# A fused attention and FFN layer on one core: first x piece in token halves, a shorter run of zero products, a full-tile count, and the float16 products first behind the last value products

## The chip, the cores and the metric

The kernel runs on one core of one Trainium2 chip. The metric is device time in microseconds (us) of that core, the median of several runs. TensorE (PE in the profile) does matrix products and loads its weights separately (PEld); VectorE is DVE, ScalarE is ACT, GpSimd is POOL, and SyncE (SP) issues most of the DMA transfers. A "q" behind an engine's name (SPq, ACTq) is its instruction queue, where transfers are issued.

## The reference

The input x has 4 x 2048 tokens of 256 features. One layer is computed, in float32:

```
Q = x @ W_q.T ; K = x @ W_k.T ; V = x @ W_v.T
S = (Q K^T within chunks of 32 tokens) * mask     # mask[i,j] = decay^(i-j) for i >= j, else 0
O = S V                                           # also within the chunk
attn = (sigmoid(x @ W_g.T) * O) @ W_o.T + x
x = layernorm(x + attn)
h = silu(x @ w_gate.T) * (x @ w_up.T)             # 768 hidden features, integer weights / 127
x = layernorm(x + h @ w_down.T)
```

The decay is the sigmoid of one number. The three FFN weights come as 32-bit integers between -127 and 127.

## The kernel before, in words

The 8192 tokens are worked in 16 blocks of 512 (`TB`). Within a block, features lie on the 128 partitions in two halves (`KD` = 2), and tokens run along the free dimension, or the other way round where the product needs it. The kernel is written out in program order: `in_turn` pins an instruction to its place on its engine, so the order of TensorE's products is what the Python code says.

Precision is kept by splitting. A float32 operand is written as a high part in `fp32r` (one pass on TensorE) and a low part. In attention, blocks 1 to 15 use three products of `fp32r` parts (`three`: parts hi, lo and gap). In the FFN, each product is a pair: high parts in `fp32r`, low parts in float16 (`kind` 0 and 1 in `ffn_up`; the trace names them `fg_hi`, `fg_lo` and so on). Block 0's attention is done with plain float32 products, each of which the trace shows as two matmul instructions.

**The start.** Loads are issued from two queues: SP loads the transposed x of block 0 (`xT`, two pieces of 256 KB, one per feature half), then `wq`, then the x of block 1, `wo`, the untransposed x and the integer weights; ACT loads `wg` in two pieces, `wv`, `decay` and `wk`. TensorE first runs products of zeros, whose widths stand in `WARM`, into a scratch bank `pi` (line 193). Then come the gate products of block 0 (`attn_gate`, `pg`, line 576), half of the value products (`pv`, line 618), the product of W_q and W_k (`make_m`, `pm`, line 216), the other half of `pv`, and `py` (line 597).

**The count.** Some integer weights could be too wide for the split. `wide_counter` compares the maxima of the nine weight pieces with 128 and sums the nine columns of 0 or 1 with one TensorE product `pw` (line 311) against a column of ones. It sits on TensorE between the transposes `pt` of block 0 (line 809) and the gap products `p_o` of block 1 (line 512). If the count is over zero, a slow path at the end runs.

**The loop.** For block b the loop does the FFN up-products of block b in six chunks of 128 hidden features (`hc` 0 to 5; `ffn_up`, line 879), and between them the attention of block b + 2 and b + 3: the scores `ps` (line 652), the values `po` (`attn_values`, line 688, products on a quarter of the array), the gate and value products; then the down-product `fdn` (line 734). In `ffn_up` the variable `kinds` sets which parts come first:

```
kinds = (1, 0) if hc % 2 or low_first else (0, 1)
```

so even chunks take high before low, odd chunks low before high, and two neighbouring chunks meet in the same type. For the blocks with `more` (b up to 12) chunk 4, which follows `attn_values`, is called with `low_first=True`. Block 13 is the last pass of the loop (`not more`): there the value products of block 15 stand between chunk 1 and chunk 2, and chunk 2 takes its high parts first. After the loop come blocks 14 and 15 and a hand-written tail of normalizing and storing.

Of the kernel before, what the change touches and what calls it, by code (L numbers as in the profile page):

```python
# [47 lines left out]
F32 = mybir.dt.float32  # L48
# [4 lines left out]
ALU = mybir.AluOpType  # L53

P = 128
# [3 lines left out]
TB = 512  # L59
NG = TB // P  # L60
HB = TB // 2
# [8 lines left out]
SHIFT = 2.0**12  # L70
TOP = 1.0 - 0.5 / SHIFT
WHOLE = 1.0 + 1.0 / SHIFT
WARM = 512, 256, 128


@with_exitstack
def kernel(
# [15 lines left out]
    nc = tc.nc  # L93
    NT, D = x.shape
    H = ffn_gT.shape[1]
    KD = D // P
# [4 lines left out]
    const = ctx.enter_context(tc.tile_pool(name="const", bufs=1))  # L101
# [12 lines left out]
    def in_turn(ins):  # L114
        tc.keep_in_program_order(ins)

    def bank(name):
        return psum.tile([P, TB], F32, tag="ps", name=name)


    def span(b, start):
        return slice(b * TB, (b + 1) * TB) if start is None else bass.ds(start, TB)

    def queue(start):

        return nc.sync if start is None else nc.gpsimd

    def load_xT(b, start=None, pieces=1):
        xt = xin.tile([P, KD, TB], F32, tag="xT", name=f"xT_{b}")
        src = xT[:, span(b, start)].rearrange("(k p) t -> p k t", p=P)  # L130
        n = KD // pieces
        for k in range(0, KD, n):
            queue(start).dma_start(xt[:, k : k + n, :], src[:, k : k + n, :])
        return xt

    def load_xn(b, start=None):
# [5 lines left out]
    def load_w(eng, w, name, pieces=1):  # L142
        k, n = w.shape[0] // P, w.shape[1]
        t = const.tile([P, k, n], w.dtype, tag=name, name=name)
        per = k // pieces
        for i in range(0, k, per):
            eng.dma_start(
                t[:, i : i + per, :], w.rearrange("(k p) n -> p k n", p=P)[:, i : i + per, :]
            )
        return t  # L150
# [2 lines left out]
    decay = const.tile([P, 1], F32, tag="decay", name="decay")  # L153
    xTs, xns = {}, {}
    wg = load_w(nc.scalar, w_gT, "wg", pieces=KD)
    xTs[0] = load_xT(0, pieces=KD)
    wv = load_w(nc.scalar, w_vT, "wv")
    nc.scalar.dma_start(decay, log_decay[0:1, 0:1].to_broadcast([P, 1]))
    wq = load_w(nc.sync, w_q, "wq")
# [31 lines left out]
    pi = bank("pi")  # L191
    for n in WARM:
        nc.tensor.matmul(
            pi[:, :n],
            lhsT=nc.const_aps.tensor(0.0, [P, P]),
            rhs=nc.const_aps.tensor(0.0, [P, n]),
            start=True,
            stop=True,
# [6 lines left out]
    half = const.tile([P, NG], F32, tag="half", name="half")  # L205
# [82 lines left out]
    top = const.tile([P, n_pieces], F32, tag="top", name="top")  # L288
# [13 lines left out]
    def wide_counter():  # L302

        wide = const.tile([P, top.shape[1]], F32, tag="wide", name="wide")
        in_turn(nc.vector.tensor_scalar(wide, top, EXACT, None, ALU.is_gt))
        ones = const.tile([P, 1], F32, tag="ones", name="ones")
        nc.vector.memset(ones, 1.0)

        def count_wide():
            pw = bank("pw")[:1, : top.shape[1]]  # L310
            in_turn(nc.tensor.matmul(pw, lhsT=ones, rhs=wide, start=True, stop=True))
            count = const.tile([1, 1], F32, tag="count", name="count")
            in_turn(nc.vector.tensor_reduce(count, pw, mybir.AxisListType.X, ALU.add))
            return count

        return count_wide
# [7 lines left out]
    def in_steady_turn(ins):  # L324
        if steady:
            tc.keep_in_program_order(ins)
# [233 lines left out]
    def split_v(b, x_parts):  # L560
        v = work.tile([P, NG, D], F32, tag="v", name=f"v_{b}")
        per = TB // D

        def finish(i, pb):
            in_turn(nc.scalar.copy(flat(v, slice(i * per, (i + 1) * per)), pb))

        return v, three(f"v_{b}", token_major(w_parts["wv"], x_parts), finish)

    def attn_gate(b):
        xt = xTs[b]  # L570
        sg = work.tile([P, KD, TB], F32, tag="sg", name=f"sg_{b}")
        banks = [bank(f"pg_{b}_{dc}") for dc in range(KD)]

        for ec in range(KD):
            for dc, pg in enumerate(banks):
                product = nc.tensor.matmul(  # L576
                    pg,
                    lhsT=given["wg"][:, ec, dc * P : (dc + 1) * P],
                    rhs=xt[:, ec, :],
                    start=(ec == 0),  # L580
                    stop=(ec == KD - 1),
                )
                in_turn(product)
        def gate():
            for dc, pg in enumerate(banks):
                in_turn(nc.scalar.activation(sg[:, dc, :], pg, AF.Tanh, scale=HALF))

        return sg, gate
# [275 lines left out]
    def no_more_splits():  # L864
        while late_splits:
            late_splits.pop(0)()

    def ffn_up(b, hT, uT, chunks, cols=slice(0, TB), held=False, low_first=False):

        n = cols.stop - cols.start  # L870
        for hc in chunks:
            pg = bank(f"fg_{b}_{hc}_{cols.start}")[:, :n]
            pu = bank(f"fu_{b}_{hc}_{cols.start}")[:, :n]

            kinds = (1, 0) if hc % 2 or low_first else (0, 1)
            for kind in kinds:
                for pb, w in ((pg, fg), (pu, fu)):
                    for dc in range(KD):
                        product = nc.tensor.matmul(  # L879
                            pb,  # L880
                            lhsT=w[kind][:, dc, hc * P : (hc + 1) * P],
                            rhs=hT[kind][:, dc, cols],
                            start=(kind == kinds[0] and dc == 0),
                            stop=(kind == kinds[1] and dc == KD - 1),
                        )
                        in_turn(product)
            s = work.tile([P, n], F32, tag="s", name=f"s_{b}_{hc}")
            in_turn(nc.scalar.activation(s, pg, AF.Silu, scale=SCALE / H_UP))  # L888
            no_more_splits()
            if len(uT[0]) == hc:  # L890
                for kind, dtype, tiles in zip(("hi", "lo"), (F32R, F16), uT):
                    tiles.append(
                        acts.tile([P, TB], dtype, tag=f"u_{kind}", name=f"u_{kind}_{b}_{hc}")
                    )

            def multiply(hc=hc, pu=pu, s=s):
                u = work.tile([P, n], F32, tag="u", bufs=3, name=f"u_{b}_{hc}")
                in_steady_turn(
                    nc.vector.scalar_tensor_tensor(u, pu, U_UP / H_UP, s, ALU.mult, ALU.mult)  # L899
                )  # L900
                hi, lo = uT[0][hc][:, cols], uT[1][hc][:, cols]

                def split():
                    in_steady_turn(nc.scalar.copy(hi, u))  # L904
                    in_steady_turn(nc.gpsimd.tensor_tensor(lo, u, hi.bitcast(F32), ALU.subtract))  # L905

                if lagging:
                    late_splits.append(split)
                else:
                    split()  # L910

            if held:
                return multiply
            multiply()
# [159 lines left out]
    count = count_wide()  # L1074
# [5 lines left out]
    def up_now(b, hT, uT, hc):  # L1080
        ffn_up(b, hT, uT, range(hc, hc + 1))
# [19 lines left out]
    for b in range(NB - 2):  # L1101
        n = b + 2
        m = b + 3
        more = m < NB
# [3 lines left out]
        hT = hTs.pop(b)  # L1108
        uT = ([], []) if b else uT_0
# [6 lines left out]
        multiply = ffn_up(b, hT, uT, range(1, 2), held=True)  # L1116
# [11 lines left out]
            multiply()  # L1128
        if not more:
            goT = attn_values(n, sT, v, sg)  # L1130
        multiply = ffn_up(b, hT, uT, range(2, 3), held=True)
        if b > 1:
            normalize(r_before, *scales_out, range(NG // 2))
        multiply()
# [4 lines left out]
            moving = move_h(b + 1, hs[b + 1])  # L1139
        if not more:  # L1140
            go_parts, go_gaps = token_parts(goT, f"go_{n}")
        multiply = ffn_up(b, hT, uT, range(3, 4), held=True)
        if b > 1:
            normalize(r_before, *scales_out, range(NG // 2, NG))
        multiply()
# [2 lines left out]
        if more:  # L1148
            sT_next = attn_scores(m, yT)
            goT = attn_values(n, sT, v, sg)  # L1150
            multiply = ffn_up(b, hT, uT, range(4, 5), held=True, low_first=True)
            go_parts, go_gaps = token_parts(goT, f"go_{n}")
            if b == 0:
                cast_fd(1, range(1))
            multiply()
            go_gaps()
            v_next, v_rest = split_v(m, x_parts)
            sg_next, g_rest = split_gate(m, x_parts)
            v_rest()
            if b == 0:  # L1160
                cast_fd(1, range(1, 2))
            up_with_cast(b, hT, uT, 5, 1, range(2, 3))
        else:
            up_now(b, hT, uT, 4)
            go_gaps()
        r_before = r_out
        if more:
# [26 lines left out]
        else:  # L1194
            multiply = ffn_up(b, hT, uT, range(5, KH), held=True)
# [19 lines left out]
    per = NG // 2  # L1215
    cols = [slice(i * per * P, (i + 1) * per * P) for i in range(2)]
    uT_last = [], []
    uT = [], []
# [19 lines left out]
    for i in range(2):  # L1238
        groups = range(i * per, (i + 1) * per)
        multiply = ffn_up(last - 1, hTs[last - 1], uT, range(3 + i, 4 + i), held=True)  # L1240
# [263 lines left out]
    with tc.If(wide_any > 0, preferred_fallthrough_block=False):  # L1504
# [10 lines left out]
        for w in (ffn_gT, ffn_uT, ffn_dT):  # L1515
            weights.append([])
            for src in int_pieces(w):
                t = room.pop(0).rearrange("p (k n) -> p k n", n=D)
# [52 lines left out]
```

## Time and profile before

| what | value |
|---|---|
| median of 3 runs | 489.17 us (489.13 to 489.43) |
| the profiled execution's own time | 489.44 us |
| its span, first to last instruction | 487.8 us |
| mean granted TensorE clock over the span | 0.999 |
| TensorE busy | 481.4 us, 99% of the span |
| ACT, DVE, POOL busy | 374.5, 338.7, 281.2 us |
| TensorE busy after 482.40 us | 0.13 us |

The profile is one execution. A row of the timeline gives a start, a duration, the engine, the line, the operation, output and inputs, and a count where equal neighbours were merged. Matmuls overlap one another: a row's duration includes the time that a result takes to come out, so the pace of the engine is read from the distance between starts, not from the durations. The waits list who waited for whom, with total, number of times and longest, in us.

### The profile page before, as it was taken

The numbers are of one execution on the slowest core, as the hardware profiler recorded it, in microseconds if no ns is written. First come the engines' busy times: TensorE is split into PE (matmuls) and PEld (weight loads), VectorE is DVE, ScalarE is ACT, GpSimd is POOL, SyncE is SP. The second block draws the span as 40 slices with busy tenths as digits, with TensorE's granted clock in tenths as the row PEclk, the third lists the DMA queues.
The fourth block names the chain that finished last, engine by engine and source line by source line (L and its number), as shares of the span: only waits on it lengthen the run. The fifth ranks groups of instructions, "written<-read, shape, count | busy, mean of one in ns | idle before, by whom it ended". The sixth has DMA issues, their size and how long they took to land.

```text
span 487.8 us, 12289 instructions
## 1 busy us (share of the span) xinstructions
PE 481.4 (99%) x4760; PEld 382.3 (78%) x4760; DVE 338.7 (69%) x795; ACT 374.5 (77%) x699; POOL 281.2 (58%) x285
## 2 busy tenths in 40 slices
PE   9999999999999999999999999999999999999995
PEld 5787787887868878687887868878687887868674
DVE  4687958687575876757677575875757677567656
ACT  4878687687877878688687877878688787786845
POOL 3835755555735565464555735566465555657764
PEclk9999999999999999999999999999999999999999
DMA  8820411211403123131411403123132211103102
GB/s 258 253 92 7 131 45 51 80 46 42 133 22 110 44 59 118 31 101 54 118 47 39 134 25 110 45 80 94 27 105 54 79 44 38 53 20 112 35 14 83
DMA packets 43323, 36.99 MB, mean 76 GB/s; under 512 B 4864, under 2 KB 39168, under 8 KB 43264
## 3 DMA queue, kind: packets, MB, share of 16 engines
q1 hardware_dynamic: 42144, 35.28, 24.4%
q10 hardware_dynamic: 1120, 0.92, 0.6%
q8 instruction: 38, 0.62, 0.5%
q14 instruction: 21, 0.17, 0.1%
HBM read 20.45 MB, written 8.39 MB: 59 GB/s over the span
## 4 chain that ended last, share of the span: by engine, by line
PE 98%; DMA 1%; DVE 0%; ACT 0%; issue 0%
PE fg L879 18%; PE fu L879 18%; PE fdn L734 14%; PE p_v L512 9%; PE p_o L512 9%; PE p_y L490 9%; PE p_g L490 9%; PE po L688 4%; PE ps L652 2%; PE fdn L953 2%; PE fdn L1313 1%; PE pg L576 1%; DMA wg<-in_w_gT_dram 1%; PE pa L767 1%; PE pv L618 1%; PE py L597 1%
## 5 line engine op out<-in xcount | busy, mean ns | idle before, releaser
L905 POOL TENSOR_TENSOR u_lo<-u,u_hi 128x512 f16<-128x512 f32 (+1 forms) x98 | 129.4, 1325 | 96.5 <-ACT u_hi L904 95.4
L899 DVE SCALAR_TENSOR_TENSOR u<-fu,s 128x512 f32<-128x512 f32 (+1 forms) x98 | 66.1, 675 | 84.7 <-ACT s L888 82.5
L888 ACT ACTIVATE s<-fg 128x512 f32<-128x512 f32 (+1 forms) x98 | 57.4, 585 | 48.1 <-PE fg L879 48.1
L904 ACT CAST u_hi<-u 128x512 fp32r<-128x512 f32 (+1 forms) x98 | 59.4, 606 | 32.8 <-DVE u L899 32.8
L879 PE MATMUL fg<-hT_hi,fg_hi 128*128 128x512 f32 (+1 forms) x196 | 72.4, 451 | 0.0
L879 PE MATMUL fu<-hT_hi,fu_hi 128*128 128x512 f32 (+1 forms) x196 | 60.5, 390 | 0.0
L879 PE MATMUL fg<-hT_lo,fg_lo 128*128 128x512 f16 (+1 forms) x196 | 58.2, 379 | 0.0
L879 PE MATMUL fu<-hT_lo,fu_lo 128*128 128x512 f16 (+1 forms) x196 | 57.5, 375 | 0.0
L471 POOL TENSOR_TENSOR go_lo<-goT,go_hi 128x512 fp32r<-128x512 f32 x30 | 44.6, 1506 | 18.2 <-ACT go_hi L470 18.2
L477 DVE SCALAR_TENSOR_TENSOR go_gap<-go_hi,goT 128x512 fp32r<-128x512 f32 x30 | 48.2, 1645 | 0.8 <-ACT go_hi L470 0.7
L471 POOL TENSOR_TENSOR x_lo<-xT,x_hi 128x512 fp32r<-128x512 f32 x30 | 37.8, 1283 | 14.6 <-ACT x_hi L470 14.6
L734 PE MATMUL fdn<-fd_hi,u_hi 128*128 128x256 f32 x312 | 44.6, 285 | 0.0
L879 PEld LDWEIGHTS fg<-hT_hi,fg_hi 128*128 128x128 f32 x196 | 35.7, 190 | 10.3
L879 PEld LDWEIGHTS fu<-hT_hi,fu_hi 128*128 128x128 f32 x196 | 36.6, 188 | 8.4
L788 DVE TENSOR_TENSOR h<-p_o,x 128x512 f32<-128x512 f32 x30 | 19.3, 685 | 32.8 <-PE p_o L512 28.9
L734 PEld LDWEIGHTS fdn<-fd_hi,u_hi 128*128 128x128 f32 x312 | 38.9, 188 | 0.3
L734 PE MATMUL fdn<-fd_lo,u_lo 128*128 128x256 f16 x312 | 38.6, 274 | 0.0
L856 POOL TENSOR_TENSOR hT_lo<-hT,hT_hi 128x512 f16<-128x512 f32 x28 | 35.4, 1284 | 4.3 <-ACT hT_hi L855 4.3
L879 PEld LDWEIGHTS <-fu_lo 128*128 128x128 f16 x196 | 19.2, 98 | 22.2
L734 PEld LDWEIGHTS <-u_lo 128*128 128x128 f16 x312 | 28.4, 98 | 3.9
L424 ACT ACTIVATE h<-h,shift_h,scale_h 128x256 f32<-128x256 f32 x52 | 27.0, 589 | 2.2 <-DVE shift_h L387 0.8
L879 PEld LDWEIGHTS <-fg_lo 128*128 128x128 f16 x196 | 13.1, 98 | 19.2 <-issue 12.8
(175 smaller groups left out, 1042.7 us busy)
## 6 DMA issues: line engine op xcount, KB each, us to landing
x<-in_x_dram SPq DMA_DIRECT2D x16, 512.0 KB, 3.9
xT<-in_xT_dram SPq DMA_DIRECT2D x15, 512.0 KB, 4.7
hT<-sq SPq DMA_DIRECT2D x224, 32.0 KB, 1.9
out_dram<-r SPq DMA_DIRECT2D x13, 512.0 KB, 3.3
out_dram<-r SPq DMA_DIRECT2D x7, 128.0 KB, 1.7
fg_int<-in_ffn_gT_dram SPq DMA_DIRECT2D x3, 256.0 KB, 7.9
fu_int<-in_ffn_uT_dram SPq DMA_DIRECT2D x3, 256.0 KB, 7.1
fd_int<-in_ffn_dT_dram SPq DMA_DIRECT2D x3, 256.0 KB, 5.9
```

The source lines that it names most:

```text
L424: nc.scalar.activation(r[:, g, :], r[:, g, :], AF.Identity, bias=shift[:, g : g + 1], scale=scale[:, g : g + 1],)
L471: in_turn(nc.gpsimd.tensor_tensor(lo[:, k, :], t[:, k, :], whole, ALU.subtract))
L477: nc.vector.scalar_tensor_tensor(gap[:, k, :], whole, -WHOLE, t[:, k, :], ALU.mult, ALU.add)
L490: nc.tensor.matmul(pb, lhsT=a[kind][:, k, i * P : (i + 1) * P], rhs=b[kind][:, k, :], start=kind + k == 0, stop=True, skip_group_check=True,)
L512: nc.tensor.matmul(pb[:, j * D : (j + 1) * D], lhsT=b[kind][:, k, g * P : (g + 1) * P], rhs=a[kind][:, k, :], start=kind + k + j == 0, sto ...
L734: product = nc.tensor.matmul(pb[:, j * D : (j + 1) * D], lhsT=part[:, g * P : (g + 1) * P], rhs=w, start=(i == 0), stop=(i == len(terms) - 1),
L856: nc.gpsimd.tensor_tensor(in_order[1], whole, in_order[0].bitcast(F32), ALU.subtract)
L879: product = nc.tensor.matmul(pb, lhsT=w[kind][:, dc, hc * P : (hc + 1) * P], rhs=hT[kind][:, dc, cols], start=(kind == kinds[0] and dc == ...
L888: in_turn(nc.scalar.activation(s, pg, AF.Silu, scale=SCALE / H_UP))
L899: nc.vector.scalar_tensor_tensor(u, pu, U_UP / H_UP, s, ALU.mult, ALU.mult)
L904: in_steady_turn(nc.scalar.copy(hi, u))
L905: in_steady_turn(nc.gpsimd.tensor_tensor(lo, u, hi.bitcast(F32), ALU.subtract))
```

## The change

- `WARM` goes from three zero products (512, 256 and 128 columns) to two (512 and 128).
- The first piece of block 0's `xT` is loaded in two transfers of 256 tokens (128 KB each) instead of one of 512 tokens. The second piece is unchanged.
- The gate products of block 0 that use this piece are done by token halves: four products of 256 columns instead of two of 512. Those of the second piece are unchanged. Only the very first product into a bank starts it; the others add.
- The count's product uses a 128 x 128 tile of the constant 1.0 in place of a 128 x 1 tile `ones` that was filled by a memset; its result then fills 128 partitions, of which the first is read.
- In `ffn_up`, `low_first` now exchanges the order of the parts in even and odd chunks alike, where before it made every chunk low-first. In the last pass of the loop (block 13), chunks 2, 3 and 4 are called with it: low-high, high-low, low-high, instead of high-low, low-high, high-low. For the other blocks nothing changes, since only chunk 4 has the flag there, and it is even.

```diff
-WARM = 512, 256, 128
+WARM = 512, 128
...
-    def load_xT(b, start=None, pieces=1):
+    def load_xT(b, start=None, pieces=1, first_by=1):
         xt = xin.tile([P, KD, TB], F32, tag="xT", name=f"xT_{b}")
         src = xT[:, span(b, start)].rearrange("(k p) t -> p k t", p=P)
         n = KD // pieces
         for k in range(0, KD, n):
-            queue(start).dma_start(xt[:, k : k + n, :], src[:, k : k + n, :])
+            per = TB // (1 if k else first_by)
+            for t in range(0, TB, per):
+                piece = slice(k, k + n), slice(t, t + per)
+                queue(start).dma_start(xt[:, *piece], src[:, *piece])
         return xt
...
-    xTs[0] = load_xT(0, pieces=KD)
+    xTs[0] = load_xT(0, pieces=KD, first_by=2)
...
-        ones = const.tile([P, 1], F32, tag="ones", name="ones")
-        nc.vector.memset(ones, 1.0)
 
         def count_wide():
-            pw = bank("pw")[:1, : top.shape[1]]
+            pw = bank("pw")[:, : top.shape[1]]
+            ones = nc.const_aps.tensor(1.0, [P, P])
             in_turn(nc.tensor.matmul(pw, lhsT=ones, rhs=wide, start=True, stop=True))
             count = const.tile([1, 1], F32, tag="count", name="count")
-            in_turn(nc.vector.tensor_reduce(count, pw, mybir.AxisListType.X, ALU.add))
+            in_turn(nc.vector.tensor_reduce(count, pw[:1, :], mybir.AxisListType.X, ALU.add))
             return count
...
-        for ec in range(KD):
+        halves = [slice(0, HB), slice(HB, TB)]
+        for ec, tokens in [(0, half) for half in halves] + [
+            (ec, slice(0, TB)) for ec in range(1, KD)
+        ]:
             for dc, pg in enumerate(banks):
                 product = nc.tensor.matmul(
-                    pg,
+                    pg[:, tokens],
                     lhsT=given["wg"][:, ec, dc * P : (dc + 1) * P],
-                    rhs=xt[:, ec, :],
-                    start=(ec == 0),
-                    stop=(ec == KD - 1),
+                    rhs=xt[:, ec, tokens],
+                    start=ec + tokens.start == 0,
+                    stop=True,
+                    skip_group_check=True,
                 )
...
-            kinds = (1, 0) if hc % 2 or low_first else (0, 1)
+            kinds = (1, 0) if hc % 2 != low_first else (0, 1)
...
-        multiply = ffn_up(b, hT, uT, range(2, 3), held=True)
+        multiply = ffn_up(b, hT, uT, range(2, 3), held=True, low_first=not more)
...
-        multiply = ffn_up(b, hT, uT, range(3, 4), held=True)
+        multiply = ffn_up(b, hT, uT, range(3, 4), held=True, low_first=not more)
...
         else:
-            up_now(b, hT, uT, 4)
+            ffn_up(b, hT, uT, range(4, 5), low_first=True)
             go_gaps()
```

## The prediction, as it was put on record

> **What bounds the kernel now.** I read the page first, its busy times and its chain.
>
> ```profile
> span 487.8 us, 12289 instructions
> PE 481.4 (99%) x4760; PEld 382.3 (78%) x4760; DVE 338.7 (69%) x795; ACT 374.5 (77%) x699; POOL 281.2 (58%) x285
> ...
> PE 98%; DMA 1%; DVE 0%; ACT 0%; issue 0%
> ```
>
> TensorE is the bound, nearly without a gap: 481.4 of 487.8 us. The last products start at 482.14, and 5.3 us of normalizing and storing follow that no edit touches. So a gain on TensorE passes to the end, and what other engines or queues gain does not count. What can be won lies at the start and in the distances between products. The chain of waits in the first 20 us shows the start:
>
> ```profile
> 0.97 3.46 DMA wg<-in_w_gT_dram
> 4.43 0.04 issue
> 4.47 4.06 PE pg L576 x8
> 8.53 1.73 PE pv L618 x8
> ```
>
> The first real product waits for a transfer, by name the first piece of wg, until 4.43. Before that TensorE multiplies zeros; narrow windows of the timeline show these and the clock:
>
> ```profile
> 1.00 3.32 PE L193 MATMUL pi<-const-float32-0.0 128*128 128x512 f32 x6 [1.00 <-PEq L1556]
> 4.63 0.34 PEld L576 LDWEIGHTS pg<-xT,wg 128*128 128x128 f32 x1
> 5.36 0.19 PEld L576 LDWEIGHTS pg<-xT,wg 128*128 128x128 f32 x1 [0.39 <-issue]
> ```
>
> The same weight load takes 0.34 us at 4.63 and 0.19 at 5.36: until a moment between, TensorE runs at half speed. The PEclk row reads full from the first slice, but the trace's own clock record begins at 5.22 us; its second and last entry is half clock for 3.41 us from 486.5. From 5.22 to 486.5 are 141 times 3.41 us. So the clock is decided at steps of 3.41 us, and 5.22 is the first step after a stretch (1.81 to 5.22) in which TensorE was busy for 3.26 of 3.41 us.
>
> For the other edits I read the timeline at their places: the count,
>
> ```profile
> 43.75 1.03 PE L809 MATMUL pt<-ident,h 128*128 128x128 f32 x8
> 44.71 0.20 PE L311 MATMUL pw<-wide,ones 128*1 128x9 f32 x2
> 44.84 0.62 PE L512 MATMUL p_o<-wo_gap,go_gap 128*128 128x256 f32 x3
> ```
>
> and the products behind the values, in block 13 (high parts first) and in block 12 (low parts first):
>
> ```profile
> 432.10 1.16 PE L688 MATMUL po<-sT,v 64*64 64x64 f32 x64
> 433.19 0.73 PE L879 MATMUL fg<-hT_hi,fg_hi 128*128 128x512 f32 x2
> 433.76 0.63 PE L879 MATMUL fu<-hT_hi,fu_hi 128*128 128x512 f32 x2
> ```
> ```profile
> 409.86 1.16 PE L688 MATMUL po<-sT,v 64*64 64x64 f32 x64
> 410.95 0.60 PE L879 MATMUL fg<-hT_lo,fg_lo 128*128 128x512 f16 x2
> 411.39 0.60 PE L879 MATMUL fu<-hT_lo,fu_lo 128*128 128x512 f16 x2
> ```
>
> **The change part by part.**
>
> *Token halves and gate by halves.* Single packets of the trace: one of 2 KB (a row of xT) holds a DMA engine 84 ns, one of 1 KB (a row of wg) 46 ns, and the SP and ACT queues alternate on each of 16 engines. From 3.0 us, when wg's packets have begun to flow, to 3.845, when its last starts, each engine takes 6.5 rounds of 84 + 46 = 130 ns. With xT rows of 1 KB a round is 92 ns: 0.60 instead of 0.845, so wg lands 0.25 us earlier, at 4.18. The first half of xT has half the bytes of what landed at 4.24 and is there before. The first product then starts at about 4.22 instead of 4.47. Ends: no gain, if the early stalls of the queues decide (up to 0.95 us on single packets); 0.57, if the start moves to 3.9. I take 0.25. Until 5.22 TensorE runs at half speed, so 0.25 us of earlier start is worth 0.13 at the end (0 to 0.29). The gate's first piece becomes eight instructions of 256 columns for four of 512. The 256-column pv rows stand 0.216 us apart at full clock, the 512-column pg rows 0.429: 4 x (0.432 - 0.429) = 0.01 us. Their loads of 0.19 (cold 0.34) hide beneath passes of 0.216 (cold 0.43). The second half's bytes stand next in the queue and land by about 4.6, needed at 5.6; the second piece landed at 5.27, needed at 6.2 or later.
>
> *One transfer more.* SP issues one DMA more (0.4 us of SP); xT's second piece and wq go out 0.44 later. Before, eight transfers go out and the ninth waits for the first landing: SP's queue waits show
>
> ```profile
> SPq L133 <- DMA wg<-in_w_gT_dram: 2.1, 1, 2.1
> ```
>
> With one more in front, wk on ACT's queue can become the ninth and wait until 4.2 instead of going out at 2.90. Behind it on ACT stand the table load (3.41 to 4.69), the one-column Sigmoid (4.70) and wg_hi (5.57): they slip by 1.3, 1.3 and about 0.65 us, and POOL's wg_lo with wg_hi. ACT then idles for the decay until 8.19, and POOL until 11.47, so this is hidden. wk lands at 8.9 and is first loaded at 9.88; its packets stand behind wv's and decay's in the same queue, so an issue 1.3 later shifts it by a few tenths at most. Cost 0; without that cover, see rival 3. The x of block 1 goes out when an early transfer lands, at 4.0 to 4.4 instead of 4.44, and its user x_hi (10.77) is safe. The integer weights are each issued behind another landing, by at most about 1 us; fg_int lands near 16.4 and is first read at 21.1. Cost 0.
>
> *Fewer zero products.* The 256-column product took 0.85 us (starts 2.835 and 3.262, the next at 3.689). The zeros end at 3.47 instead of 4.32. As the data come at 4.22 at the earliest value that I take, this itself frees nothing; it only makes a hole from 3.47 to 4.22. Here a rule weighs against the change. The Trainium skill, "TensorE: Matmul & The Clock Gate", section "Part 1: The HAM clock gate", says that the clock stays half until a window of about 3.4 us, free-running, has been one of sustained activity. The row agrees on the length. It doesn't say how much idling a window may hold. In this trace 24% busy (the window ending at 1.81, with work from 1.00) was too little and 96% was enough; after the change it would be 3.26 - 0.75 + the old hole of 0.15 = 2.66 us, 78%. Read strictly, the rule costs one more window at half speed: 3.41 / 2 = 1.71 us. Read by the row alone, with the point anywhere between 24 and 96%, the chance to miss is (96 - 78) / (96 - 24) = 25%, and 35% if the data come no earlier (71%). I take no loss as the likeliest, and the loss as the main rival.
>
> *The count.* From the last transpose (start 44.509) to the second p_o product (45.067) are 0.558 us: the one-column load starts only at 44.710, when the transposes are through, and p_o's load (0.19) starts together with its product instead of ahead. In a full tile the loads can go ahead as between the transposes, 0.108 us apart: two steps for pw, one for p_o, one of 0.117 make 0.44. Gain 0.11. The same page, section "LDWEIGHTS (loading the stationary operand)", speaks against it: a load takes columns / 1.2 ns, so 128 columns for one is 2 x 106 ns more, a loss of 0.2. The rows have 79 and 82 ns for the one-column loads, so they are not nearly free, and the price lies in the order; I take 0.11 gain, ends -0.2 and 0.12. The memset dropped is 0.06 us of DVE beside the zeros: nothing.
>
> *Float16 behind the values.* The two fg products take 433.756 - 433.188 = 0.568 where high parts come first, and 411.392 - 410.950 = 0.442 where low ones do. An undisturbed high pair takes 0.467 (436.90), a low one 0.432: the high weights' load is exposed by 0.10, the low ones' by 0.01. The rest of the order: chunks 2 to 5 took 1.910 + 1.801 + 1.809 + 1.797 = 7.317 us. From like rows the new order is 1.809 (block 12, chunk 4), 1.809, 1.801, and 1.807 for chunk 5, which now begins with a change of type: 7.226. Gain 0.09. In both orders fg is complete two products before the chunk's end, so ACT and DVE get it as before.
>
> *Sum:* 0.13 - 0.01 + 0.11 + 0.09 = 0.32 us. The profiled execution's 489.44 (span 487.8 and 1.6 around it) becomes 489.12; it stood 0.27 above the median, so the median goes from 489.17 to 488.85.
>
> **The rivals.**
>
> 1. *The clock is released a step late (0.35).* The hole before the first product keeps the window below the point that counts; the next step is at 8.63. Loss 1.71, less the 0.32: 490.56 us, slower. It decides as soon as the point lies above about 78%. For it: the hole grows from 0.15 to 0.75 us, and the skill asks for sustained work. Against it: work covers the larger part on both sides. Its own range is 490.2 to 490.9.
> 2. *The data come no earlier (0.08).* If wg is held by stalls and not by alternation, the start stays at 4.47; only count and values gain, 0.2: 488.97.
> 3. *wk too late (0.06).* If the whole 1.28 us of its later issue reached its landing, it would come at 10.2, and pm, needed 0.13 sooner at 9.75, would hold TensorE 0.45 us: 489.3. For over 0.2% it has to be about 1 us later still (0.02).
> 4. *Other order (0.08).* One more transfer and one memset less can re-plan unpinned instructions, mostly on POOL and SP. No wait of TensorE is there to be removed, so a gain of 1 us has no place that I know: 0.06 above that to the fast side, for what I overlooked; 0.02 slow.
>
> That the order change fails to reach its place is excluded by the code: only chunk 4, an even one, has the flag elsewhere.
>
> **How the numbers follow.** The likeliest is all three gains with the clock on time (0.43): 488.85, own range 488.6 to 489.1. A measurement of this kernel can tell about 0.2%, 0.98 us: below 488.19 is faster, above 490.15 slower. Same: 0.43 + 0.08 + 0.04 of rival 3 = 0.55. Slower: 0.35 + 0.02 + 0.02 = 0.39. Faster: 0.06. The range has to hold rival 1, so it runs from 488.4 (start at 3.9 and both small gains full, 488.67, less the 0.3 by which runs differ) to 490.9.
>
> **What would show it.** The first pg row at 4.2 and not 4.47, and loads of 0.19 from 5.2 on: the start is right. Loads of 0.34 until 8.6 and a later start of pv: rival 1. The p_o product 0.33 us behind the last transpose and the next 0.11 on, and a pair of 0.44 behind po in block 13: the two small gains. A wait of pm's load for wk: rival 3. The prediction is wrong if TensorE's work from 60 to 400 us changes its length, or the tail after the last product.

## The result, and the profile after

The changed kernel is slower: 495.31 us (median of 4 runs, 494.86 to 495.42) against 489.15 (4 runs, 488.90 to 489.43), a ratio of 1.0117 with a 95% interval of 1.0104 to 1.0130. The prediction had 488.85 and a range that ended at 490.9.

The page of the changed kernel, the lines that answer to those of before:

```profile
span 493.1 us, 12292 instructions
PE 484.3 (98%) x4762; PEld 385.0 (78%) x4762; DVE 338.5 (69%) x794; ACT 375.5 (76%) x699; POOL 281.6 (57%) x285
...
PE 96%; DMA 2%; DVE 0%; ACT 0%; issue 0%
```

The bound is still TensorE, but two things grew. Its busy time rose by 2.9 us with two products more. And the chain of waits gives 2% to transfers, where it was 1%. So a part of the loss is waiting, and a part is the same work at a slower pace. They lie in different places.

**The start.** The timeline of TensorE (start, duration, engine, line, operation, output and inputs, count; in brackets the idle time just before, and what ended it):

```profile
3.87 2.72 PE L581 MATMUL pg<-xT,wg 128*128 128x256 f32 x8 [0.39 <-DMA wg<-in_w_gT_dram]
7.41 1.95 PE L581 MATMUL pg<-xT,wg 128*128 128x512 f32 x4 [0.82 <-DMA xT<-in_xT_dram]
9.20 1.89 PE L624 MATMUL pv<-wv,xT 128*128 128x256 f32 x8
11.94 1.99 PE L219 MATMUL pm<-wk,wq 128*128 128x256 f32 x8 [0.85 <-DMA wk<-in_w_k_dram]
```

The first gate product starts at 3.87 instead of 4.47, earlier than forecast. But two waits follow that were not there before: 0.82 us for the second piece of xT, and 0.85 for wk. pv starts at 9.20 (before 8.36) and pm at 11.94 (before 10.09), so the 0.6 us won have become a loss of 1.85. The list of transfers in the first 16 us (transfer, queue, count, KB each, median us from issue to landing) says why:

```profile
xT<-in_xT_dram SPq DMA_DIRECT2D x1, 256.0 KB, 5.4
wk<-in_w_k_dram ACTq DMA_DIRECT2D x1, 256.0 KB, 8.1
```

The first of these is xT's second piece. It takes 5.4 us; before, the two pieces took 3.9 in the median. It went out at 1.86 instead of 1.41 and landed at 7.27 instead of 5.27. wk takes 8.1 instead of 6.0: out at 3.84 instead of 2.90, landed at 11.89 instead of 8.91. The chain of waits up to 16 us (start, duration, what), its middle:

```profile
3.84 8.05 DMA wk<-in_w_k_dram
...
11.94 1.99 PE pm L219 x8
```

wk is now the ninth transfer; it goes out when the first piece of wg has landed, and then it decides the start.

**The loop.** The value products `po` come once in a block, so their starts measure a block's length. Two rows of before, then the same two of after:

```profile
116.46 1.16 PE L688 MATMUL po<-sT,v 64*64 64x64 f32 x64
380.52 1.16 PE L688 MATMUL po<-sT,v 64*64 64x64 f32 x64
```
```profile
118.77 1.16 PE L694 MATMUL po<-sT,v 64*64 64x64 f32 x64
384.69 1.16 PE L694 MATMUL po<-sT,v 64*64 64x64 f32 x64
```

They are nine blocks apart: 264.06 / 9 = 29.340 us a block before, 265.92 / 9 = 29.547 after. Each block takes 0.207 us more, though no edit touches a product in it. The groups of the down-product, high and low parts, before and after the change (busy us, mean ns):

```profile
L734 PE MATMUL fdn<-fd_hi,u_hi 128*128 128x256 f32 x312 | 44.6, 285 | 0.0
L734 PE MATMUL fdn<-fd_lo,u_lo 128*128 128x256 f16 x312 | 38.6, 274 | 0.0
```
```profile
L740 PE MATMUL fdn<-fd_hi,u_hi 128*128 128x256 f32 x312 | 45.6, 288 | 0.0
L740 PE MATMUL fdn<-fd_lo,u_lo 128*128 128x256 f16 x312 | 38.6, 273 | 0.0
```

Only the fp32r rows, here the high parts, are longer. By mean distance between starts (57.58 to 410 us of the span), the high down-products stand 126.2 ns apart instead of 123.0, the value and output products of the attention 119.5 instead of 117.8, the 512-column gate products 233 instead of 231. Float16 products keep their 109 and 216 ns.

From the rows of `po` and the last product the sum is: up to the first `po` (25.42 before, 27.41 after) +1.99; from there to 57.58 (59.47) -0.10; from there to 409.86 (414.35) +2.60; from there to the last products, 482.14 (486.99), +0.36. That is +4.85.

**The end.** The last store takes 3.5 us from its issue to the end of the span instead of 3.1, which makes the span's 5.2. The store itself lands as fast as before, but the span now ends 1.38 us behind its landing instead of 0.96. SP's records show why: at the end SP waits on eight DMA semaphores (counters that a transfer raises when it has landed), in a fixed order and 0.06 us apart. The one that comes last belongs to the last of these eight waits before and to the first of them after, so seven more steps follow the landing. All traces below agree: 1.38 or 1.39 us in the eight kernels that issue one more transfer on SP's or ACT's queue (the changed one, 3, 5, 6, 10, 11, 12 and 13), 0.95 or 0.96 in all others. So the added transfer costs 0.42 us there too.

**The two small edits.** The count, and the products behind block 15's values:

```profile
45.74 1.03 PE L815 MATMUL pt<-ident,h 128*128 128x128 f32 x8
...
46.76 1.07 PE L514 MATMUL p_o<-wo_gap,go_gap 128*128 128x256 f32 x7
```
```profile
437.88 0.60 PE L885 MATMUL fg<-hT_lo,fg_lo 128*128 128x512 f16 x2
438.32 0.59 PE L885 MATMUL fu<-hT_lo,fu_lo 128*128 128x512 f16 x2
```

From the transposes to the gap products are 1.02 us instead of 1.09 (to the second gap product the gain is 0.10), and the first pair behind the values takes 0.44 instead of 0.57. Both small gains are in the trace.

### The profile page after: what moved, and what is told of

The parts are those of the page before. It is cut to its first block, busy times and chain, and to the rows that moved or that the text cites. A ratio compares the mean times of both kernels' runs of the same rounds, so it can differ in the third digit from the quotient of the medians.

```text
span 493.1 us, 12292 instructions
## 1 busy us (share of the span) xinstructions
PE 484.3 (98%) x4762; PEld 385.0 (78%) x4762; DVE 338.5 (69%) x794; ACT 375.5 (76%) x699; POOL 281.6 (57%) x285
## 4 chain that ended last, share of the span: by engine, by line
PE 96%; DMA 2%; DVE 0%; ACT 0%; issue 0%
PE fg L885 18%; PE fu L885 17%; PE fdn L740 15%; PE p_v L514 9%; PE p_o L514 9%; PE p_y L492 9%; PE p_g L492 9%; PE po L694 4%; PE ps L658 2%; PE fdn L959 2%; DMA wk<-in_w_k_dram 2%; PE fdn L1319 1%; PE pa L773 1%; PE py L603 1%; DMA wg<-in_w_gT_dram 1%; PE pm L219 0%
## 5 line engine op out<-in xcount | busy, mean ns | idle before, releaser
L740 PE MATMUL fdn<-fd_hi,u_hi 128*128 128x256 f32 x312 | 45.6, 288 | 0.0
L740 PEld LDWEIGHTS fdn<-fd_hi,u_hi 128*128 128x128 f32 x312 | 39.9, 189 | 0.3
L388 POOL TENSOR_SCALAR minus_out<-rstd_out 128x4 f32<-128x4 f32 x12 | 2.7, 223 | 44.8 <-DVE rstd_out L386 44.8
```

The source lines that it names most:

```text
L740: product = nc.tensor.matmul(pb[:, j * D : (j + 1) * D], lhsT=part[:, g * P : (g + 1) * P], rhs=w, start=(i == 0), stop=(i == len(terms) - 1),
```

## The experiments

The change drops one tile of 4 bytes a partition, `ones`. The addresses in the built programs show what this does: constants that are allocated ahead of it stay, and everything allocated behind it (xT, hT, u, the parts of the sums) lies 32 bytes nearer (xT from 73600 to 73568). The theory for the loop is that this shift alone slows the fp32r products. Its rival is that one of the edits does. For the start the theory is the added transfer; the rivals are named with the runs. Each kernel was timed in turn with the kernel before on the same chip. The release of the clock falls at another moment in each run (3.9 to 7.6 us in most of the traces below), and half of it passes into the time: the kernel before took from 488.84 to 490.51 over all its runs. So tenths of a microsecond are read from the traces, and times only decide from about 0.2% on.

**1 and 2. The kernel before, with later tiles 32 and 64 bytes further.** One unused tile, then two, behind `ones`:

```diff
+        pad = const.tile([P, 1], F32, tag="pad", name="pad")
+        nc.vector.memset(pad, 1.0)
```

> The kernel before with one unused 4-byte tile added behind the tile of ones (and its memset), so that every tile allocated after it lies 32 bytes further on; nothing else changes. Theory A (addresses): the fp32r products between block 1 and block 13 lose what they lost in the changed kernel, about 2.7 us (489.2 to 491.9), and the distances of float16 products stay; the start keeps the order of before: first pg product at 4.47, pm at 10.1. Rival B (the drift follows from the shifted start or from another order of the engines, not from addresses): no change, 489.2. Rival C (the late transfers at the start come from misplaced destinations too): also pm later by 1 to 2 us, 493.5 to 494.

> The same with two unused 4-byte tiles, so that later tiles lie 64 bytes further on. Theory A in the form that the place within 64 bytes decides: no change, 489.2 (within 0.3 us). If any shift of the later tiles against the earlier ones costs, as theory A would also allow: again about 491.9. Rival B: 489.2 here and in the run with 32 bytes.

Measured: 490.18 against 489.78, 1.0008 [0.9999, 1.0016], and 491.05, 1.0033 [1.0020, 1.0045]. Blocks took 29.367 and 29.447 us. Unused tiles alone change the pace, but by other amounts than the shift the other way: the 2.7 us that the theory expected from any 32 bytes did not come.

**3. The changed kernel with the addresses of before.** The same unused tile, put where `ones` was.

> The changed kernel with an unused 4-byte tile (and its memset) in the place of the tile of ones, so that all tiles lie where they lay before. Theory A with the queues as the cause at the start: the drift of 2.7 us is gone, the late second piece of xT (wait of about 1 us) and the late wk (about 1 us) stay: 489.15 + 1.95 - 0.2 = about 490.9 to 491.5. Rival C (destinations make the transfers late): start good too, 488.5. Rival B: 495.3 as the changed kernel.

Measured: 492.09 against 489.78, 1.0053 [1.0041, 1.0066]. The loop is back:

```profile
118.83 1.16 PE L696 MATMUL po<-sT,v 64*64 64x64 f32 x64
236.19 1.16 PE L696 MATMUL po<-sT,v 64*64 64x64 f32 x64
```

Four blocks in 117.36 us are 29.34 each (a single later block took 29.44), and the high down-products are back at 285 ns. The start stays as late as in the changed kernel: wk lands at 12.34 and pm starts at 12.38. So loop and start are two causes, and the loop's goes away with the tile put back.

**4. The small edits alone.** The kernel before with the full-tile count, the unused tile, and the new order in block 13; three zero products and whole pieces stay.

```diff
-        ones = const.tile([P, 1], F32, tag="ones", name="ones")
-        nc.vector.memset(ones, 1.0)
+        pad = const.tile([P, 1], F32, tag="pad", name="pad")
+        nc.vector.memset(pad, 1.0)
...
-            kinds = (1, 0) if hc % 2 or low_first else (0, 1)
+            kinds = (1, 0) if hc % 2 != low_first else (0, 1)
```

> The kernel before with only the full-tile count (and an unused tile in place of the ones, so that addresses stay) and the new order of parts in block 13; three zero products, first piece of xT whole, gate whole. As predicted for these two parts: 0.11 + 0.09 = 0.2 us faster, 488.95. If neither is worth anything: 489.15.

Measured: 489.80 against 489.78, 1.0002 [0.9994, 1.0010], too little for the time to tell. The trace has the count 0.08 faster. Block 15's values need a closer reading. The timeline of this kernel, then of the kernel before, up to the low part of the down-product that follows chunk 5:

```profile
434.10 0.60 PE L885 MATMUL fg<-hT_lo,fg_lo 128*128 128x512 f16 x2
...
444.16 1.05 PE L959 MATMUL fdn<-fd_lo,u_lo 128*128 128x256 f16 x8
```
```profile
443.23 1.05 PE L953 MATMUL fdn<-fd_lo,u_lo 128*128 128x256 f16 x8
```

Chunks 2 to 5 take 7.235 us instead of 7.317, the gain that was forecast. But the 24 fp32r products behind them (16 of `p_o`, 8 of `fdn`) now stand 118 ns apart, where they stood 113. From the first fg to the low down-product are 444.16 - 434.10 = 10.06, against 443.23 - 433.19 = 10.04: the gain is given back at once. All kernels with the old order that keep the addresses show 113 here, all with the new order and the same addresses 118. At these addresses the order of the products thus sets the pace of later fp32r products too; run 9 shows that it does not at others.

**5. wk ahead of decay.** The changed kernel with the unused tile; the rival is that wk's place as ninth is what costs.

```diff
-    nc.scalar.dma_start(decay, log_decay[0:1, 0:1].to_broadcast([P, 1]))
     wq = load_w(nc.sync, w_q, "wq")
     wk = load_w(nc.scalar, w_k, "wk")
+    nc.scalar.dma_start(decay, log_decay[0:1, 0:1].to_broadcast([P, 1]))
```

> The changed kernel with addresses as before (unused tile) and one step moved: ACT issues wk before the decay, so that wk is among the first eight transfers and the decay is the ninth that waits for a landing. Theory (the ninth place makes wk late): wk goes out by 2.9, lands by 9, TensorE does not wait for it; the pm step of 1.4 us seen with addresses restored is gone, about 490.7 instead of 492.1. The decay comes later, and ACT's Sigmoid with it, hidden. Rival (rows of 1 KB and the early x of block 1 slow all transfers from 4.5 us on): wk is late wherever it stands, pm still waits about 1 us, 492.

Measured: 492.67 against 489.51, 1.0082 [1.0057, 1.0106]: nothing won. wk went out at 2.37, and pm no longer waited. The chain shows where the wait went:

```profile
3.88 7.99 DMA decay<-in_log_decay_dram
...
15.62 0.48 ACT m_sb L227
...
16.14 1.12 PE py L605 x2
```

Now decay, of 0.5 KB, is the ninth. It needs 8 us as well, landing at 11.87, and ACT does its Sigmoid, a table load, `sg` and `x_hi` behind it before it can copy pm to `m_sb`, for which py waits. With the further transfer in front, what is ninth in the program's order on ACT's queue landed between 11.55 and 12.34 in five kernels (the changed one, 3, 5, 10 and 11).

**6. A ninth transfer in the kernel before.** wv in two pieces, so that wk is the ninth without a further transfer in front of xT's second piece: `load_w(nc.scalar, w_vT, "wv", pieces=KD)`.

> The kernel before with wv loaded in two pieces of 128 KB: one transfer more before wk, all bytes, the first piece of xT, the gate and the zeros as before. Theory (the ninth place): wk waits for the first landing and goes out at about 4.45; it lands about 1.5 to 3 us later than 8.9, and pm waits 0.5 to 2 us: 490.3 to 491.8. Rival (the halves of xT are the cause): wk late in its issue but not in its landing, 489.8.

Measured: 490.06 against 489.51, 1.0013 [1.0006, 1.0020]. wk went out at 4.24, even later than in the changed kernel, landed at 9.14, and pm started on time (10.22). So the ninth place alone does not cost the 2 us.

**7. The whole piece, with two zero products.** Kernel 3 with the first piece in one transfer and its gate products whole. It differs from kernel 4 in the missing 256-column zero product alone. This is rival 1 by itself.

> The changed kernel with addresses as before (unused tile), the first piece of xT and its gate products whole again, but the two zero products, the count and the order in block 13 as changed. It differs from the run of small gains only in the zero product of 256 columns. If the hole in TensorE's work before the first product keeps the clock at half for one step more (rival 1 of the prediction): about 491.5. If not: 489.8, as with three zero products.

Measured: 490.85 against 489.51, 1.0028 [1.0017, 1.0040]. Two weight loads of its timeline:

```profile
9.72 0.34 PEld L581 LDWEIGHTS pg<-xT,wg 128*128 128x128 f32 x1 [0.52 <-issue]
10.45 0.19 PEld L624 LDWEIGHTS pv<-wv,xT 128*128 128x128 f32 x1 [0.40 <-issue]
```

Loads of 0.34 us until 9.72: the clock record begins at 10.32. The zeros ended at 3.47, the gate began at 4.43, and pv started at 10.88 instead of 9.38 in kernel 4 (8.36 in the kernel before). The window before, 3.50 to 6.91, held 0.93 us of the hole, so TensorE was busy for 2.48 of 3.41 us (73%), and the clock was not released. Rival 1 is real. The halves of xT shorten the hole to 0.4 us, but they do not always keep the shorter run of zeros from paying it. In kernel 3 the window from 0.80 to 4.21 was busy for 2.79 us (82%); the loads behind it still took 0.33 us, and the clock came one step later, at 7.62. With this hole filled, the window would by this sum have been 94% busy. The least busy windows that did release the clock had 86% (0.51 to 3.92 in kernel 9, 3.20 to 6.61 in kernel 11, 1.38 to 4.79 in kernel 12). So in these traces the point lies between 82 and 86%, and whether a hole costs a step depends on where the window falls.

**8. decay on POOL's queue.** To take the ninth place from both queues: `nc.gpsimd.dma_start(decay, ...)` in kernel 3.

> The changed kernel with addresses as before (unused tile) and the decay loaded from POOL's queue instead of ACT's, so that eight transfers stand on the two other queues. Theory (the ninth place makes wk late): wk goes out at 2.4, before the first landing, and is there in time; block 1's x still goes out as soon as a landing allows. pm's wait is gone: 490.3 or, where the second piece of xT comes in time too, 489.3. Rival (1 KB rows slow all transfers): the second piece and wk are late as before, 492.

Measured: 495.48 against 489.51, 1.0123 [1.0106, 1.0140], the worst of all.

```profile
9.63 3.75 PE L583 MATMUL pg<-xT,wg 128*128 128x512 f32 x4 [3.09 <-DMA xT<-in_xT_dram]
```

The second piece landed at 9.49; from 4 to 5 us the transfers together moved 35 KB, from 5 to 6 us 98. TensorE then idled so long that its clock fell back to half from 8.79 to 15.62.

**9. The count alone.** The kernel before, `ones` dropped, nothing put in its place.

> The kernel before with the full-tile count alone, as in the change: the tile of ones is gone and later tiles lie 32 bytes nearer. Zeros, transfers, gate and block 13 as before. Theory A (addresses): a block of the steady loop takes 29.55 us between its value products instead of 29.34, as in the changed kernel: 13 blocks x 0.2 = 2.6 us, less 0.08 for the count: about 2.5 slower than the kernel before, 492. Rival (the loss per block belongs to the changed start): 29.34, no change.

Measured: 492.05 against 489.84, 1.0050 [1.0031, 1.0068].

```profile
116.60 1.16 PE L687 MATMUL po<-sT,v 64*64 64x64 f32 x64
382.52 1.16 PE L687 MATMUL po<-sT,v 64*64 64x64 f32 x64
```

265.92 / 9 = 29.547, as in the changed kernel; the high down-products are at 288 ns, and TensorE ends 2.66 us later. With kernel 3 this closes the loop's part from both sides: with the tile gone it is there, with it put back it is not. What stays argued is that the addresses do it. In every run a tile came and went together with its memset on VectorE, and no run moves the addresses without one.

This kernel has block 15's old order at the addresses of the changed one. The first output product behind chunk 5 and the low down-product behind the 24, here and then in the changed kernel:

```profile
442.92 0.64 PE L511 MATMUL p_o<-wo_hi,go_hi 128*128 128x256 f32 x4
...
445.80 1.05 PE L952 MATMUL fdn<-fd_lo,u_lo 128*128 128x256 f16 x8
```
```profile
445.09 0.64 PE L514 MATMUL p_o<-wo_hi,go_hi 128*128 128x256 f32 x4
...
447.98 1.05 PE L959 MATMUL fdn<-fd_lo,u_lo 128*128 128x256 f16 x8
```

The 24 products take 2.88 and 2.89 us: the same in either order. From the first fg (435.60 and 437.88) to the low down-product are 10.20 and 10.10 us, so in the changed kernel the new order kept its 0.10.

**10. The halves alone.** The kernel before with xT's first piece in two transfers; the gate products, the zeros and the rest as before.

```diff
-    xTs[0] = load_xT(0, pieces=KD)
+    xTs[0] = load_xT(0, pieces=KD, first_by=2)
```

> The kernel before with the first piece of xT in two transfers and nothing else: the gate is whole, three zero products, addresses as before. Theory (the transfers are slowed by the halves, their order and the early x of block 1): the second piece lands at 7 to 7.6 instead of 5.3, wk at about 12 instead of 8.9, and pm waits; with the start at 4.2 about 491.5 to 492. Rival (the gate by halves or the fewer zeros bring the waits): wk and the second piece as before, 489.5.

Measured: 491.87 against 489.84, 1.0041 [1.0026, 1.0055].

```profile
3.92 8.14 DMA wk<-in_w_k_dram
...
12.10 1.99 PE pm L219 x8
```

The second piece landed at 7.57 and wk at 12.06, so one more transfer, by itself, makes the start as late as in the changed kernel. The blocks took 29.340 us. In the trace the transfers together move 180 to 290 KB a us from 4 to 8 us, where before it was 360 to 390 until 6. Single packets are held for over 1 us from 5.5 us on (up to 1.6); in the kernel before, this came from 6.1 us on (up to 1.3).

**11. Less behind the second piece.** In kernel 3 the 512 KB of block 1's x are issued behind wo instead of ahead of it. The rival is that this load, which goes out at 3.65 instead of 4.44, crowds the second piece.

> The changed kernel with addresses as before (unused tile), and on SP the 512 KB of block 1's x issued behind wo instead of before it. If the early start of that big transfer is what takes the bandwidth from the second piece, wv and wk: transfers keep over 300 KB/us until about 6 us, second piece at 5.3, wk by 9.5, pm's wait gone: about 490.3. If not: waits as with addresses restored, 492.1.

Measured: 491.73 against 489.84, 1.0042 [1.0029, 1.0056].

```profile
8.12 1.96 PE L583 MATMUL pg<-xT,wg 128*128 128x512 f32 x4 [0.88 <-DMA xT<-in_xT_dram]
```

The second piece landed at 7.98, no earlier. wk came at 11.55, just ahead of pm at 11.63, which was due only then because pv was late. This load is not the cause.

**12. Rows of 2 KB kept.** The kernel before with the first piece split by partitions (64 and 64) instead of by tokens, so that each packet stays 2 KB. The rival is the 1 KB row.

> The kernel before with the first piece of xT in two transfers of 64 partitions each: rows stay 2 KB, but SP has one more transfer at the place where the token halves have it. If the place and number of transfers slow the rest: second piece at 7 to 7.6 and wk at 11.5 to 12, about 492, as with the token halves alone. If the rows of 1 KB do it: second piece near 5.3 to 5.7, pm on time, 489.5 to 490.

Measured: 492.93 against 489.22, 1.0069 [1.0041, 1.0098]. The first product waited until 5.50 and the next piece came at 9.57. The five runs spread widely (491.13 to 495.00). So 1 KB rows are not needed for it; a further transfer ahead of the second piece on SP is enough.

**13. One more transfer on SP behind the second piece.** wq in two pieces in the kernel before.

> The kernel before with wq in two transfers of 128 KB: SP has one more transfer, behind the second piece of xT. If any further transfer on SP slows the rest: wk late, pm waits, 491 to 492. If it is only one ahead of the second piece, or the 1 KB rows: as before, 489.8.

Measured: 490.22 against 489.22, 1.0016 [1.0009, 1.0023]. The second piece landed at 5.19 and pm started on time (10.63, with the clock released at 6.36). No wait of TensorE in the trace accounts for the 0.16%, but 0.42 us of it, 0.09%, is the longer end.

**14 to 17. Further shifts, and the best version.** Unused tiles as in 1: the kernel before with later tiles 96 and 128 bytes further (one run each), then kernel 4 with its later tiles 128 and 256 bytes further than before.

> The kernel before with three unused 4-byte tiles: later tiles 96 bytes further on. Theory A without a rule: the time of a block differs again from 29.340 (0 bytes), 29.367 (32), 29.447 (64) and 29.547 (-32). If the place within 64 bytes had a say, it would be near the 32-byte run's; if it grows with the distance, over 29.45.

> The kernel before with four unused 4-byte tiles: later tiles 128 bytes further on. A block takes 29.340 us at 0 bytes, 29.367, 29.447 and 29.427 at 32, 64 and 96, 29.547 at -32. If the place within 128 bytes decided, 29.340 again; if not, some other value, by the four others 29.35 to 29.55.

> The kernel before (first piece of xT whole, gate whole, three zero products) with the full-tile count and the order of parts in block 13 as changed, and unused 4-byte tiles so that later tiles lie 128 bytes further on. From the traces: places -0.5 us, count -0.08, block 13 -0.10: together 0.7 us faster than the kernel before, 488.5 where that is at 489.2. If the single look at 128 bytes was a lucky step of the clock alone: 0.2 us, not to be told from no change.

> The same at 256 bytes further on. If places repeat every 128 bytes from the one before, a block takes 29.340 or 29.293 us; without a rule, by the six places seen, between 29.25 and 29.55: 488 to 492.

| later tiles moved by, bytes | us a block | time |
|---|---|---|
| -32 (the count alone; the changed kernel) | 29.547 | 492.05 (495.31) |
| 0 | 29.340 | 489.15 to 489.84 |
| 32 | 29.367 | 490.18 |
| 64 | 29.447 | 491.05 |
| 96 | 29.427 | 491.22, one run |
| 128 | 29.293 | 488.75, one run |
| 128, with the small edits | 29.266 | 487.73 |
| 256, with the small edits | 29.340 | 489.72 |

At 128 bytes the version with both small edits beats both kernels: 487.73 against 489.52, 0.9969 [0.9957, 0.9981], 1.8 us where 0.7 was expected. Its rows:

```profile
115.89 1.16 PE L702 MATMUL po<-sT,v 64*64 64x64 f32 x64
379.28 1.16 PE L702 MATMUL po<-sT,v 64*64 64x64 f32 x64
```

263.39 / 9 = 29.266 us a block, and the 24 products behind block 15's values are at 113 ns here, with the new order, so the gain of that edit is kept. But the blocks are quicker than in the run at 128 bytes without the edits (29.293), though their products and addresses are the same; why was not found. The two ran on different chips, but kernels at the addresses of before took 29.340 us on three chips alike. At 256 bytes the blocks are those of before (1.0005 [0.9997, 1.0013]). No period of 128 bytes or less in the offset fits these points; one of 256, with 29.340 at both ends, would, and was not tried.

## Why the prediction was wrong, step by step

- *Earlier start (0.13 of gain).* That halves bring wg earlier was right (it landed at 3.82, and at 3.89 with the halves alone), its size larger: the start was 3.87, not 4.22. It was worth nothing, since the second piece came later than the first could be used up.
- *"The second piece landed at 5.27, needed at 6.2 or later".* The first of three terms that failed. The step shifted this transfer's issue by 0.45 us and took its landing to shift by little more. It landed 2.00 later, and TensorE waited 0.82. The kernel with the halves alone shows it without any other edit.
- *"An issue 1.3 later shifts it by a few tenths at most. Cost 0"* (wk). The second term that failed. The issue was 0.94 later and the landing 2.98. Rival 3 named the place (a wait of pm's load for wk), but sized it at 0.45 and gave it 0.06; together with the second piece pm was 1.85 late. Both steps took the rate of before as given. The trace of before already held a stretch, 6.0 to 7.5 us, in which the transfers moved 124 to 148 KB a us, and it fell where nobody waited. The further transfer brings such a stretch forward to 4 us.
- *The clock (rival 1, 0.35).* It was released on time, at 5.38, since the data came at 3.87: the window that ended there was 88% busy. That is luck. By the prediction's own sum the window would have been 78% busy, and the runs put the point between 82 and 86%, so with the start that it took as likeliest the clock would have come a step later. The kernel with the whole piece and two zero products shows that loss. The Trainium skill ("TensorE: Matmul & The Clock Gate", "Part 1: The HAM clock gate") asks for sustained activity in a free-running window; the free-running part shows as release times from 3.92 to 7.62 us in kernels whose work ahead of it is nearly the same.
- *The count (0.11 of gain).* Measured 0.10 between the prediction's marks (0.456 us from the last transpose to the second gap product, instead of 0.558), though the two steps in it were 0.25 and 0.20, not 0.33 and 0.11. The same page's price of loads by columns ("LDWEIGHTS (loading the stationary operand)"), from which the prediction's estimate of 0.2 slower came, is not borne out here: the place of the load in the order counted.
- *Float16 behind the values (0.09).* Right: 0.08 to 0.10 over the four chunks, as computed from like rows, and kept in the changed kernel. But the step took the pace of the 24 fp32r products behind as fixed, and kernel 4 shows that this is not safe: at the addresses of before they took the gain back.
- *"The memset dropped is 0.06 us of DVE beside the zeros: nothing".* The third term that failed, and the costliest. A tile of 4 bytes went with the memset, and the two together were 2.7 us. The prediction's own last sentence, that it is wrong if TensorE's work from 60 to 400 us changes its length, or the tail after the last product, names the view that shows it.
- *"5.3 us of normalizing and storing follow that no edit touches".* A smaller miss: the further transfer made the end 0.42 us longer.

By time, the halves alone (1.0041, or 1.0053 in the changed kernel with its addresses restored) and the count alone (1.0050) make 1.009 to 1.010 of the 1.0117 [1.0104, 1.0130]. The traces put 2.0 us at the start and 0.4 at the end on the first, 2.7 on the second. What remains, about 0.1 to 0.2%, is of the size of the clock's free phase, and no run assigns it; time outside the span is part of it (1.7 to 2.3 us in the changed kernel's runs, 1.5 to 1.7 in the kernel before's).

Two questions stay open. Why a transfer ahead of xT's second piece on SP slows the others from 4 us on was not found: the ninth place, block 1's x and the row size are excluded, each by a run. And why fp32r products keep one of a few paces (113, 118, about 121 ns for like products) was not found either: a dropped or unused tile and the order of products both move it, and float16 products show it in none of these traces.

## What to carry to other kernels

Before trusting a sum over the edited instructions, compare the address of every tile before and after, and the length of a loop pass that no edit touches; a dropped constant can cost more than all edits together, and an unused tile is a cheap thing to sweep. Where transfers are issued close together, a further one is not priced by its bytes: take the landing of everything behind it as unknown, and ask for each what waits for it. A gain between two products counts only when the products behind them keep their pace, so read the sum at the next fixed mark, not at the end of the edit.

## What the runs showed of the hardware that was not expected

- The pace of fp32r products changes when a 4-byte tile (with its memset) is dropped or added and later tiles move in SBUF, the chip's on-chip memory: 29.266 to 29.547 us a block over shifts of -32 to 256 bytes (the lowest with the small edits), with the same float16 pace of 109 ns throughout.
- At the addresses of before it also depends on the products that ran before: 113 or 118 ns for 24 products, by the order of the parts in chunks 2 to 4 ahead of them. At -32 bytes (2.88 us for the 24) and at 128 (2.73) the order made no difference.
- With a further transfer in front, one of 0.5 KB as the ninth took 8.0 us to land, as long as one of 256 KB in the same place (8.1).
- With a 0.5 KB transfer moved to a third queue, all transfers together moved 35 and then 98 KB a us for two microseconds, where the changed kernel's moved about 250.
- The clock was not released by a window of 3.41 us that was 82% busy, and was by windows of 86%.
- One more transfer on SP's or ACT's queue near the start moved the end of the span 0.42 us further behind the last store's landing, in eight kernels of eight; the order of SP's last waits is why.
